# A start-up, a scan entry and a last output reordered in a four-layer convolution and attention kernel

## The chip, the cores and the metric

The kernel runs on one core of a Trainium2 chip, as one program. The metric is device time in microseconds of that core. The kernel before took 3007.63 us, the median of three runs (3004.27 to 3009.06). The engines are named as in the profile: PE (TensorE: matmul), PEld (its weight load), DVE (VectorE), ACT (ScalarE), POOL (GpSimd) and SP (SyncE, which here only issues DMAs). ACT issues DMAs too; an issue takes its place in ACT's own order of instructions.

## The reference

The input x is 8 images of 128 channels and 16 x 16 pixels (256 positions). Four layers follow each other:

- Layer 0: `x = x + adder2d(gn(x), W)`. gn normalises groups of 4 channels (32 groups) over the positions of an image. The adder is a 3 x 3 convolution with a distance in place of the product: `out[f] = -sum |W[f] - patch|` over 128 channels and 9 taps.
- Layer 1: a layer norm over channels, a projection to 2 x 256 channels, and three Mamba branches (forward, backward, in slices). Each takes a causal convolution of 4 taps, SiLU, a projection to a step width (delta, through softplus) and to B and C, and a selective scan of 16 states: `h = exp(delta*A)*h + delta*u*B; y = sum(h*C) + u*D`. Attention between the branches and two 3 x 3 convolutions close it.
- Layer 2: attention within an image and a mixture of 8 experts, two of them chosen.
- Layer 3: a performer of 8 layers, and a spectral layer (convolutions with 16 filters, and a sum over 3 taps) whose result is added to the state and is the output.

## The kernel before

All is fp32. Channels lie on the 128 partitions; the 8 images of 256 positions are 2048 columns, in 4 blocks (pairs of images) of 512. An fp32 matmul shows as two passes in the profile, so that one call of `E.mm` is two PE instructions.

**Layer 0** (`adder_layer`, to about 950 us). It uses |a - b| = 2 max(a, b) - a - b for some taps and |a - b| on ACT for the others. For each of the 128 filters, DVE (L450, L446) and ACT (L452) write a tile d of 128 x 2048 for each tap, from four buffers each, and PE sums d over the channels into a row of `o` (L454 to L458): `add` issues four matmuls of 32 columns, one for each block, into four groups of 32 output partitions. Two sums that depend on no filter pair are left: `px`, the sum over channels of the shifted inputs of six taps (L423 to L425), and `wsum`, the weights' sums (twelve passes: six taps with one output column each, L427). Both are read at L461 to L466, after two filters. `px` and `wsum` come ahead of the first `o` product on PE.

Ahead of these stands `start` (L315): for each pair of images DVE sums x (L333), PE averages over the group (mu), ACT writes the negative mean and the squares (L337, L339), DVE sums the squares (L341), PE averages (var), ACT takes the root (L345), DVE the reciprocal and two scalings into `shifted[1]` (L347 to L350), and copies of it give `shifted[0]` and `shifted[2]` (L351, L354). Between these PE does products that nobody reads, `meanwhile(n)`, one call being two passes.

The loads are issued at the head of `adder_layer` (L375 to L383): on ACT the first 128 columns of the constants, x's pairs 1 and 3, then, in `load_shared`, the other constants, the vectors and the rows; on SP x's pairs 0 and 2, the adder's weights w, and the weights of layer 1 (`load_weights`).

**Layer 1** begins with `first_unit` (L701) on the first pair and branch. Its order is written by hand: norm, projection, convolution, `pp` into `proj` (L759 to L763), the store of `proj`'s rows and their way back as broadcast B and C (`chunk`), then `pd` (L770), which gives delta over ACT and DVE (L774 to L786), the first decays on ACT (L827) and the first scans on DVE (L909). `spare` (L705) lies in the PSUM bank "acc", of which there is one; the scan's accumulator `acc` (L914) takes the same bank, and starts with the products of L916. The copy of `u` (L788) is the last step; the next unit's convolution (`pconv`) needs it.

The order of PE, DVE, ACT and POOL within each `manual_schedule` block is that of the program. Between the blocks the compiler's scheduler orders: of two instructions of one engine in different blocks, the one that can go first may.

**The end** (`spectral_layer`). The outputs lie in five groups of columns: group 0 (positions 0 to 31 of all images), group 1 (32 to 63), group 2 (64 to 127), and groups 3 and 4 (128 to 255, four images each), with 256, 256, 512, 512 and 512 columns. For each, PE adds three taps (L1874), DVE adds the state X (L1876) into `fin`, which has two buffers, and SP stores it (L1882).

Of the kernel before, what the change touches and what calls it, by code (L numbers as in the profile page):

```python
# [16 lines left out]
P = 128  # L17
B = 8
# [3 lines left out]
NBLK = NT // BLK  # L22
# [201 lines left out]
class Env:  # L224
# [31 lines left out]

    def load_shared(self):
        nc = self.nc
        nc.scalar.dma_start(self.cst[:, P:], self.dram["cst"][:, P:])
        nc.scalar.dma_start(self.vecs, self.dram["vecs"])  # L260
        nc.scalar.dma_start(self.rows, self.dram["rows"].partition_broadcast(P))

    def load_weights(self):
        for k, t in self.w.items():
# [42 lines left out]
MAX_TAPS = (0, 2, 4, 6, 8)  # L307
MORE_TAPS = (7,)
MORE = tuple(r for r in range(FG) if r % 10 in (0, 3, 6))
JOINED = (0, 2)  # L310
PX_TAPS = (4, 7, 0, 6, 2, 8)
# [3 lines left out]
def start(E, pool, psum, x, shifted):  # L315

    nc = E.nc
    spare = psum.tile([P, P], F32, tag="px", name="spare")

    def meanwhile(n):  # L320

        for _ in range(n):
            E.mm(spare, E.ones, E.ones)

    def small(name):
        return pool.tile([P, B], F32, tag=name, name=name)

    s1, neg_mu, s2, rs = (small(n) for n in ("s1", "neg_mu", "s2", "rs"))
    sq = pool.tile([P, B, L], F32, tag="sq", name="sq0")
    pairs = [slice(2 * i, 2 * i + 2) for i in range(NBLK)]  # L330
    meanwhile(6)
    for b in pairs:
        nc.vector.tensor_reduce(s1[:, b], x[:, b, :], AX.X, ALU.add)  # L333
        mu = psum.tile([P, 2], F32, tag="st", name="mu0")
        E.mm(mu, E.c("group"), s1[:, b])
        meanwhile(2 if b is not pairs[-1] else 1)
        nc.scalar.copy(neg_mu[:, b], mu)  # L337
        for i in range(b.start, b.stop):
            nc.scalar.activation(sq[:, i, :], x[:, i, :], AF.Square, bias=neg_mu[:, i : i + 1])  # L339
    for b in pairs:  # L340
        nc.vector.tensor_reduce(s2[:, b], sq[:, b, :], AX.X, ALU.add)  # L341
        var = psum.tile([P, 2], F32, tag="st", name="var0")
        E.mm(var, E.c("group"), s2[:, b])
        meanwhile(1 if b is not pairs[-1] else 2)
        nc.scalar.activation(rs[:, b], var, AF.Sqrt, bias=E.eps, scale=-1.0)  # L345
    for b in pairs:
        nc.vector.reciprocal(rs[:, b], rs[:, b])  # L347
        for i in range(b.start, b.stop):
            dst = shifted[1][:, i, 1:17, :].rearrange("p h w -> p (h w)")
            nc.vector.tensor_scalar(dst, x[:, i, :], neg_mu[:, i : i + 1], rs[:, i : i + 1], ALU.add, ALU.mult)  # L350
        nc.scalar.copy(shifted[0][:, b, 1:17, 1:16], shifted[1][:, b, 1:17, 0:15])  # L351
    for i, b in enumerate(pairs):
        op = nc.vector.tensor_copy if i < 2 else nc.scalar.copy
        op(shifted[2][:, b, 1:17, 0:15], shifted[1][:, b, 1:17, 1:16])  # L354


def adder_layer(E):
# [7 lines left out]
    nc, tc = E.nc, E.tc  # L365
    with ExitStack() as ctx:
# [7 lines left out]

        x = last.tile([P, B, L], F32, tag="x", name="x0")  # L375
        nc.scalar.dma_start(E.cst[:, :P], E.dram["cst"][:, :P])
        for i in range(NBLK):
            two = slice(2 * i, 2 * i + 2)
            (nc.scalar if i % 2 else nc.sync).dma_start(x[:, two, :], E.dram["x"][two].rearrange("b c s -> c b s"))
        w = p.tile([P, 9, P], F32, tag="w", name="w0")  # L380
        nc.sync.dma_start(w, E.dram["adder"])
        E.load_shared()
# [9 lines left out]
        neg = p.tile([P, 2, FG], F32, tag="neg", name="neg")  # L392
# [13 lines left out]
        def tap(k):  # L406
            kh, kw = divmod(k, 3)
            return shifted[kw].rearrange("p b h w -> p b (h w)")[:, :, kh * 16 : kh * 16 + L]

        def add(out, lhsT, src, start, stop, blocks=range(NBLK)):  # L410

            for i in blocks:
                E.mm(out[i * FG : (i + 1) * FG, :], lhsT, src[:, 2 * i : 2 * i + 2, :], start, stop)

        px = ps.tile([P, BLK], F32, tag="px", name="px0")
        xsum = p.tile([P, BLK], F32, tag="xsum", name="xsum")
        with tc.manual_schedule(engines={nc.tensor.engine, nc.vector.engine, nc.scalar.engine}):
            nc.scalar.preload_act_table_set(SQRT)
            start(E, p, ps, x, shifted)

            wsum = [ps.tile([P, 1], F32, tag="st", name="wsum") for _ in range(2)]
            weights = [(pw, taps, k) for pw, taps in zip(wsum, (MAX_TAPS, MORE_TAPS)) for k in taps]
            for n, k in enumerate(PX_TAPS):  # L423
                for i in range(NBLK):
                    add(px, neg[:, int(k in MORE_TAPS), :], tap(k), n == 0, n == len(PX_TAPS) - 1, (i,))  # L425
                    for pw, taps, t in weights[2 * i : 2 * i + 2] if n == 0 else ():
                        E.mm(pw, w[:, t, :], E.ones[:, 0:1], start=t == taps[0], stop=t == taps[-1])  # L427

# [2 lines left out]
        for g in range(NG):  # L433
            out = po.tile([P, BLK], F32, tag="o", name="o")
# [100 lines left out]
def _scans(E, ctx, F):  # L535
# [7 lines left out]
    nc, tc = E.nc, E.tc  # L543
    w_x, w_dt = E.w["xproj"], E.w["dtproj"]
    one = ctx.enter_context(tc.tile_pool(name="l1one", bufs=1, reuse_waits="tile"))
    two = ctx.enter_context(tc.tile_pool(name="l1two", bufs=2, reuse_waits="tile"))
# [154 lines left out]
    def first_unit(k, s, p, new, pre, sig, proj):  # L701
# [29 lines left out]
        t = xn[p] = two.tile([P, UT], F32, tag="xn", name="xn1")  # L731
# [20 lines left out]
        t, pc = sig[:, 0, :], pc.rearrange("p b l -> p (b l)")  # L752
# [15 lines left out]
        for h, (tag, scratch) in enumerate((("f", "ln_xc"), ("cs", "ln_rstd"))):  # L768
            pd = ps.tile([P, UT], F32, tag=tag, name="pd")
            E.mm(pd, w_dt[:, k, h * P : (h + 1) * P], proj[0:DTR, :])  # L770
            one_e = one.tile([P, UT], F32, tag=scratch, name="one_e")
            halves.append((pd, delta[:, h, :], pre[:, h, :], sig[:, h, :], one_e))

        for h, (pd, d, e, r, one_e) in enumerate(halves):  # L774
            db = E.v("db" + s, h)
# [91 lines left out]
    with tc.manual_schedule(engines={nc.tensor.engine, nc.vector.engine, nc.scalar.engine, nc.gpsimd.engine}):  # L867
        new, *rest = tiles()
        got[0].update(new)
        first = first_unit(*units[0], new, *rest)  # L870
        next(first)
        for c in range(2):
            chunk("bs", 0, c)
            chunk("cs", NST, c)
        dbs[0] = three.tile([P, 2, UT], F32, tag="db", name="dbu")
        for h in range(2):
            next(first)
            nc.vector.tensor_mul(dbs[0][:, h, :], new["du"][:, h, :], row("bs", 0))
            decays(h)
            if h == 0:  # L880
                rows_of_c(0)
        inputs(1)
        next(first)
        decays(2)
# [7 lines left out]
    with tc.manual_schedule(engines={nc.tensor.engine, nc.vector.engine, nc.scalar.engine, nc.gpsimd.engine}):  # L892
        for r in range(states):
            i, n = divmod(r, NST)
            k, s, p = units[i]
# [905 lines left out]
def spectral_layer(E, W, out):  # L1801
# [7 lines left out]
    nc, tc = E.nc, E.tc  # L1809
    with ExitStack() as ctx:  # L1810

        def enter(name, bufs, **kw):
            return ctx.enter_context(tc.tile_pool(name=name, bufs=bufs, reuse_waits="tile", **kw))

        ugp = enter("sug", 2)
        two = enter("stwo", 2)
# [7 lines left out]
        groups = []  # L1824
        for i in reversed(range(4)):
            lo, hi = ends[i + 1], ends[i]
            n = min(B, BLK // (hi - lo))
# [6 lines left out]
        def at(tile, offset, *dims):  # L1834
            a = tile[:]
            return bass.AP(a.tensor, a.offset + offset, [list(a.ap[0]), *([s, n] for s, n in dims)])

        for step in range(NK // KG):
# [8 lines left out]
            for b in range(B):  # L1847
                for q in range(2):
                    p4 = pu.tile([P, KG, 2, HL], F32, tag="u", name="p4")

                    taps = at(W.T, step * KG * TW + 1, (TW, KG), (HL + 1 - q, 2), (1, HL))
# [4 lines left out]
            for k in range(KG):  # L1856
                for s in range(2):
                    for j, (i, lo, hi, b0, b1) in enumerate(groups):
# [4 lines left out]
                            start=step == 0 and k == 0 and s == 0,  # L1863
                            stop=False,
# [3 lines left out]
        nc.sync.dma_start(mu, E.dram["Mu"].rearrange("i d t e -> d i t e"))  # L1868
        W.running(E, [mu[:, i].rearrange("p t e -> p (t e)") for i in range(4)])
        X = E.X.rearrange("p (b l) -> p b l", l=L)  # L1870
        for j, (i, lo, hi, b0, b1) in enumerate(groups):
            for k in range(TAPS):
                tap = u[:, b0:b1, TAPS - 1 - k + lo : TAPS - 1 - k + hi]
                E.mm(acc[j], mu[:, i, k, :], tap.rearrange("p b (i q) -> p b q i", q=2), start=False, stop=k == TAPS - 1)  # L1874
            fin = two.tile([P, b1 - b0, hi - lo], F32, tag="fin", name="fin")
            nc.vector.tensor_tensor(  # L1876
                fin.rearrange("p b (i q) -> p b q i", q=2),
                X[:, b0:b1, lo:hi].rearrange("p b (i q) -> p b q i", q=2),
                acc[j],
                ALU.add,  # L1880
            )
            nc.sync.dma_start(out[b0:b1, :, lo:hi].rearrange("b c s -> c b s"), fin)  # L1882


def program(tc, dram, out, cols):
    with ExitStack() as ctx:
        E = Env(ctx, tc, dram, cols)
        adder_layer(E)
        mamba_layer(E)
        E.early.close()  # L1890
        with ExitStack() as tail:
            W = Spectral(E, tail)
            performer_layer(E, W)
            spectral_layer(E, W, out)
# [25 lines left out]
```

## Time and profile before

| | |
|---|---|
| median of three runs | 3007.63 us (3004.27 to 3009.06) |
| profiled execution, its own time | 3000.94 us |
| its span, first to last instruction | 2999.2 us |
| PE busy | 2854.1 us (95%), 16404 instructions |
| DVE busy | 2419.8 us (81%) |
| ACT busy | 2273.2 us (76%) |
| POOL busy | 699.6 us (23%) |
| o products of the adder (L289) | 921.5 us, 8512 passes |
| first s1 sum (L333) starts | 4.02 us |
| first o product starts | 24.83 us |
| first scan (L909) starts | 978.91 us |
| last fin (L1876) starts | 2995.26 us |

Lines of the page give an engine, a line, what is written and read, a count, busy time and the mean of one. "Idle" is what the engine waited just before, with what ended it. L289 is the helper `E.mm`, so matmuls are told apart by their tiles. The chain of work that ended last is followed back from the last instruction. All sums below are made on the profiled execution.

### The profile page before, as it was taken

The page shows a single profiled execution, that of the slowest core. Times are in us where ns is not written, and L with a number is a line of the kernel's source. Part 1 is how long each engine was busy: PE and PEld are TensorE (multiplying, and loading weights), DVE is VectorE, ACT ScalarE, POOL GpSimd, SP SyncE. Part 2 cuts the span into 40 slices and gives each one's busy share as a digit, 9 for nine tenths or more (in the row PEclk, how much of TensorE's full clock was granted, in tenths as well). Part 3 has the DMA queues.
Part 4 walks back from the last instruction along what each step waited for, and adds up shares of the span by engine and source line. Part 5 has one row for each costly group of instructions (what it writes and reads, how often), then busy time and mean ns, then how long its engine had stood idle before and what let it go on. Part 6 is the DMA issues. An engine that isn't in the chain of part 4 may idle for free.

```text
span 2999.2 us, 41845 instructions
## 1 busy us (share of the span) xinstructions
PE 2854.1 (95%) x16404; PEld 1275.4 (43%) x16404; DVE 2419.8 (81%) x3398; ACT 2273.2 (76%) x2744; POOL 699.6 (23%) x415
## 2 busy tenths in 40 slices
PE   9999999999999788998898998999999999999999
PEld 4222222222223333443343454455655555654444
DVE  8999999999997999999899658887777787784110
ACT  8999999999997777778777435578778778777332
POOL 0000000000000889998999400000000000000100
PEclk9999999999999999999999999999999999999999
DMA  2000000000000444344344200000000000001100
GB/s 68 1 1 5 1 1 5 1 2 5 1 1 16 169 149 148 135 149 141 133 157 137 84 29 1 14 1 14 14 14 1 14 14 1 14 1 53 43 29 14
DMA packets 39482, 133.46 MB, mean 44 GB/s; under 512 B 7522, under 2 KB 10732, under 8 KB 37748
## 3 DMA queue, kind: packets, MB, share of 16 engines
q1 hardware_dynamic: 38164, 129.46, 12.5%
q8 instruction: 129, 2.11, 0.3%
q10 hardware_dynamic: 1120, 1.32, 0.1%
q14 instruction: 69, 0.57, 0.1%
HBM read 127.88 MB, written 1.84 MB: 43 GB/s over the span
## 4 chain that ended last, share of the span: by engine, by line
PE 70%; DVE 16%; ACT 7%; POOL 3%; issue 3%; DMA 1%; DVEq 0%; ACTq 0%; POOLq 0%
PE o L289 30%; PE p L289 10%; DVE st L909 5%; PE acc L289 5%; PE g L289 4%; PE conv L289 3%; PE pc L289 2%; PE var L289 2%; PE pf L289 2%; POOL dbu L814 2%; PE pq L289 2%; PE pconv L289 1%; PE pn L289 1%; PE pa L289 1%; ACT da L827 1%
## 5 line engine op out<-in xcount | busy, mean ns | idle before, releaser
L289 PE MATMUL o<-d,sel 128*32 128x512 f32 x8512 | 921.5, 593 | 2.1 <-DVE d L446 1.2
L452 ACT ACTIVATE d<-sh,w 128x2048 f32<-128x2048 f32 x472 | 899.3, 1993 | 25.4 <-PE o L289 25.1
L450 DVE TENSOR_SCALAR d<-sh,w 128x2048 f32<-128x2048 f32 x592 | 718.4, 1281 | 11.0 <-PE o L289 10.9
L814 POOL TENSOR_TENSOR dbu<-du,bs 128x1024 f32<-128x1024 f32 x191 | 446.4, 2363 | 975.6 <-DVE du L786 970.1
L289 PEld LDWEIGHTS o<-d,sel 128*32 128x32 f32 x8512 | 278.6, 110 | 644.2 <-issue 523.0
L909 DVE TENSOR_TENSOR_SCAN st<-da,dbu 128x512 f32<-128x512 f32 x384 | 446.2, 1206 | 17.9 <-POOL dbu L814 13.8
L289 PE MATMUL acc<-st,cst 128*128 128x512 f32 x768 | 375.4, 621 | 52.8 <-DVE st L920 52.6
L827 ACT ACTIVATE da<-delta,neg_a 128x510 f32<-128x510 f32 x384 | 256.8, 684 | 79.1 <-DVE st L909 73.8
L289 PEld LDWEIGHTS acc<-st,cst 128*128 128x128 f32 x768 | 144.6, 196 | 252.7 <-issue 144.0
L920 DVE TENSOR_TENSOR st<-st,pcs 128x1024 f32<-128x1024 f32 x168 | 205.2, 1221 | 18.9 <-ACT pcs L819 1.6
L446 DVE SCALAR_TENSOR_TENSOR d<-sh,w,d 128x2048 f32<-128x2048 f32 x88 | 206.8, 2350 | 1.9
L1855 ACT COPY ug<-p 128x512 f32<-128x512 f32 x128 | 74.9, 585 | 136.7 <-PE p L289 136.7
L1173 ACT ACT_TABLE_LOAD x134 | 171.9, 1283 | 2.4
L1396 POOL TENSOR_TENSOR lw<-lw,turn 128x640 f32<-128x640 f32 x8 | 10.0, 1255 | 685.6 <-DVE turn L1395 592.6
L819 ACT COPY pcs<-cs 128x512 f32<-128x512 f32 x168 | 97.7, 582 | 54.2 <-DVE st L920 48.4
L289 PE MATMUL conv<-pad,f 128*128 128x512 f32 x288 | 135.0, 596 | 0.9 <-ACT pad L1071 0.5
L289 PE MATMUL p<-un,lw 128*128 128x512 f32 x256 | 123.7, 605 | 3.8 <-DVE un L1467 2.1
L289 PE MATMUL p<-g,lw 128*128 128x512 f32 x256 | 116.4, 597 | 3.9 <-ACT g L1181 3.9
L289 PE MATMUL p<-T,H 128*128 128x512 f32 x256 | 113.0, 600 | 0.8 <-DVE H L1784 0.8
L289 PE MATMUL g<-ug,me 128*128 128x512 f32 (+1 forms) x320 | 112.0, 509 | 0.0
L1181 ACT ACTIVATE ex<-ex 128x352 f32<-128x352 f32 x128 | 62.4, 494 | 51.6 <-DVE ex L1664 50.4
L289 PE MATMUL pf<-lw,rk 128*128 128x352 f32 x256 | 97.2, 476 | 0.5 <-DVE ek L1614 0.3
(366 smaller groups left out, 3898.6 us busy)
## 6 DMA issues: line engine op xcount, KB each, us to landing
bs<-rows SPq DMA_DIRECT2D x96, 512.0 KB, 3.8
cs<-rows SPq DMA_DIRECT2D x96, 512.0 KB, 4.6
m<-in_Mphi SPq DMA_DIRECT2D x8, 1024.0 KB, 4.9
lw<-in_layers SPq DMA_DIRECT2D x8, 948.0 KB, 4.7
f<-in_fuse SPq DMA_DIRECT2D x2, 1152.0 KB, 9.9
T<-in_T SPq DMA_DIRECT2D x1, 2064.0 KB, 7.4
diag<-in_diag SPq DMA_DIRECT2D x1, 1920.0 KB, 7.5
total<-sums SPq DMA_DIRECT2D x16, 64.0 KB, 2.0
```

The costliest lines, as they stand in the source:

```text
L289: self.nc.tensor.matmul(out, lhsT=lhsT, rhs=rhs, start=start, stop=stop)
L446: nc.vector.scalar_tensor_tensor(d, tap(k), wk, d, ALU.max, ALU.add)
L450: nc.vector.tensor_scalar(d, tap(k), wk, None, ALU.max)
L452: nc.scalar.activation(d, tap(k), AF.Abs, scale=-1.0, bias=wk)
L814: nc.gpsimd.tensor_tensor(dbs[r], got[r // NST]["du"], bc(row("bs", r), 1, 2), ALU.mult)
L819: nc.scalar.copy(pcs[r], row("cs", r))
L827: nc.scalar.activation(das[g % 3][:, :, 1:], d[:, :, 1:], AF.Exp, scale=a)
L909: nc.vector.tensor_tensor_scan(st[:, h, :], da, dbs[r][:, h, :], 0.0, ALU.mult, ALU.add)
L920: nc.vector.tensor_tensor(st, st, bc(pcs[r][:, :], 1, 2), ALU.mult)
L1173: S.tc.keep_in_program_order(S.nc.scalar.preload_act_table_set(name))
L1181: S.nc.scalar.activation(out, src, func, **kw)
L1855: nc.scalar.copy(dst, p4)
```

## The change

Six edits:

1. x is loaded in eight pieces of one image each, the even ones from SP and the odd ones from ACT, in place of four pairs.
2. The other constants, the vectors and the rows are issued from SP, behind x and w.
3. The last two unread products of `start` (after the fourth var) are left out.
4. The weights' sums are all issued ahead of px; px no longer takes the blocks one by one in its first tap.
5. `first_unit` issues 13 unread products (26 passes) behind the two `pd`.
6. The output groups are finished in the opposite order: 4, 3, 2, 1, 0.

```diff
     def load_shared(self):
         nc = self.nc
-        nc.scalar.dma_start(self.cst[:, P:], self.dram["cst"][:, P:])
-        nc.scalar.dma_start(self.vecs, self.dram["vecs"])
-        nc.scalar.dma_start(self.rows, self.dram["rows"].partition_broadcast(P))
+        nc.sync.dma_start(self.cst[:, P:], self.dram["cst"][:, P:])
+        nc.sync.dma_start(self.vecs, self.dram["vecs"])
+        nc.sync.dma_start(self.rows, self.dram["rows"].partition_broadcast(P))
...
         E.mm(var, E.c("group"), s2[:, b])
-        meanwhile(1 if b is not pairs[-1] else 2)
+        meanwhile(1 if b is not pairs[-1] else 0)
...
-        for i in range(NBLK):
-            two = slice(2 * i, 2 * i + 2)
-            (nc.scalar if i % 2 else nc.sync).dma_start(x[:, two, :], E.dram["x"][two].rearrange("b c s -> c b s"))
+        for b in range(B):
+            (nc.scalar if b % 2 else nc.sync).dma_start(x[:, b, :], E.dram["x"][b])
...
-        def add(out, lhsT, src, start, stop, blocks=range(NBLK)):
+        def add(out, lhsT, src, start, stop):
 
-            for i in blocks:
+            for i in range(NBLK):
                 E.mm(out[i * FG : (i + 1) * FG, :], lhsT, src[:, 2 * i : 2 * i + 2, :], start, stop)
...
-            weights = [(pw, taps, k) for pw, taps in zip(wsum, (MAX_TAPS, MORE_TAPS)) for k in taps]
+            for pw, taps in zip(wsum, (MAX_TAPS, MORE_TAPS)):
+                for k in taps:
+                    E.mm(pw, w[:, k, :], E.ones[:, 0:1], start=k == taps[0], stop=k == taps[-1])
             for n, k in enumerate(PX_TAPS):
-                for i in range(NBLK):
-                    add(px, neg[:, int(k in MORE_TAPS), :], tap(k), n == 0, n == len(PX_TAPS) - 1, (i,))
-                    for pw, taps, t in weights[2 * i : 2 * i + 2] if n == 0 else ():
-                        E.mm(pw, w[:, t, :], E.ones[:, 0:1], start=t == taps[0], stop=t == taps[-1])
+                add(px, neg[:, int(k in MORE_TAPS), :], tap(k), n == 0, n == len(PX_TAPS) - 1)
...
             halves.append((pd, delta[:, h, :], pre[:, h, :], sig[:, h, :], one_e))
+        meanwhile(13)
...
-        for j, (i, lo, hi, b0, b1) in enumerate(groups):
+        for j, (i, lo, hi, b0, b1) in reversed(list(enumerate(groups))):
             for k in range(TAPS):
```

## The prediction

> **What bounds the kernel now.** I read the chain of work that ended last first, by stages, because the edits touch four short stretches: 0 to 26 us, 968 to 983 us, and the last 15 us.
>
> The start, in that chain (start us, length us, what):
>
> ```profile
> 13.83 1.06 PE spare L289 x4
> 14.89 1.85 PE px L289 x2
> 16.74 0.82 PE wsum L289 x4
> 17.56 0.98 PE px L289 x2
> 18.53 0.54 PE wsum L289 x4
> 19.07 0.97 PE px L289 x2
> 20.04 0.54 PE wsum L289 x4
> 20.58 4.84 PE px L289 x41
> ```
>
> TensorE carries the chain from 9.9 us on, and after px come the o products back to back: over the whole adder stage o sat idle 2.1 us (the page's first group). DVE had its four d tiles ready at 21.1 and then waited 5.84 us for o; ACT waited 3.67. So every us by which px ends earlier is a us of the kernel, until px ends before about 19 us, where DVE's tiles are no longer there.
>
> Why the norm ahead of it is late, from the timeline:
>
> ```profile
> 5.14 0.33 ACTq L261 DMA_DIRECT2D rows<-in_rows  x1
> 5.51 1.28 ACT L418 ACT_TABLE_LOAD   x1 [5.51 <-DMA x<-in_x]
> 9.03 0.69 DVE L333 TENSOR_REDUCE s<-x 128x2 f32<-128x512 f32 x1 [2.60 <-DMA x<-in_x]
> ```
>
> Two delays: ACT's table load stands behind six DMA issues (rows goes out at 5.14, with the landing of the second x piece at 5.12; vecs at 3.42, with the landing of cst at 3.41; SP's fifth issue at 4.01, its first landing at 4.02: a queue seems to have four loads under way), and the fourth x pair lands only at 9.0, 7.3 us after its issue, where the others took 3.3 to 3.9.
>
> The Mamba entry, again in the chain:
>
> ```profile
> 968.09 0.43 PE spare L289 x2
> 968.52 0.04 issue
> 968.57 1.12 PE acc L289 x2
> 969.69 1.07 PE pd L289 x2
> ...
> 981.44 0.52 ACT u L788
> 981.96 0.04 issue
> 982.00 5.98 PE pconv L289 x8
> ```
>
> proj is ready at 968.71 (copy at 968.13, 0.58), yet pd starts at 969.62 by the timeline: the two acc products of L916, emitted later in the program, have slipped in ahead of it.
>
> The clock there, by stages (the last three columns are granted clock, DMA share, GB/s):
>
> ```profile
> 972.00:974.00 2.00, 0.66 (x2) 0.00 (x0) 1.48 (x4) 1.48 (x4) 0.00 (x0) 0.75 1.06 260
> 974.00:982.00 8.00, 0.00 (x0) 0.00 (x0) 7.79 (x12) 3.57 (x7) 0.42 (x1) 0.50 0.54 181
> 982.00:986.00 4.00, 4.00 (x5) 1.85 (x6) 3.86 (x5) 1.83 (x3) 4.00 (x2) 0.50 0.13 49
> ```
>
> The clock halves at 973.0 and comes back at 986.7; pconv runs at half speed.
>
> **What the skill says.** "TensorE: Matmul & The Clock Gate", Part 1: the array is at half clock by default or after an idle window of about 3.4 us, and at full clock after a busy one; the windows run free. The trace agrees: 128x512 passes start 0.85 us apart at 982 and 0.43 later, and the changes at 973.0, 986.7, 1075.4, 1078.8 lie multiples of 3.41 us apart. Carried back, that grid gives 17.3 us, where px changes from 1.92 to 1.05 us a pair. "DMA: Bandwidth & Descriptors", queues, rings and completion order: each DMA engine takes turns between queues, packet by packet. This fits the late x pair: w's rows of 4.6 KB on SP's queue against x's of 1 KB; from 5 to 7 us SP's queue moved 0.55 MB and ACT's 0.19. "TensorEngine Tiling (Array Packing)", key properties: a change of tiling mode drains the array; px is 128x32 and wsum 128x128, and each wsum's weight load after a px sat idle 0.84 us.
>
> **The change, part by part.**
>
> *Loads.* Eight pieces of 128 KB replace four of 256. DMA moved 0.38 MB/us from 3 us on, 0.2 MB before. With equal packets on both queues (cst's 128 are 0.5 KB), pair 0 needs 0.46 MB: 3.9 us; pairs 1 and 2: 4.6 and 5.3. The last piece is ACT's fifth load, issued at 3.42 when cst has landed; w waits on SP for x's first landing (3.9), so it reaches the engines about when x is done; behind it on SP stand only loads of the next sentences. I take 6.5 us (5.8 to 8) for pair 3, against 9.0. w (0.59 MB, behind it) lands at about 7.3, needed at 10.9. cst, vecs and rows go behind it on SP; first needed at 36 us (L466, L469), in POOL's center (nothing waits until 952) and at 946 us. Cost nothing; weights for 952 us and later have 900 us.
>
> *ACT.* One issue after 3.42 instead of two: table load 3.8 to 5.1, neg_mu at 5.1 instead of 6.80. ACT takes 0.985 us a pair: pairs end at 6.2, 7.2, 8.2, 9.15; before, 11.56. DVE's last s2 ends at 9.9, not 12.28 (-2.4), then its own order (four times reciprocal and two scalings, 0.85) gives sh1 complete at 13.3 and the first d at 13.9 against 16.21. ACT's copies of sh0 end at 13.9.
>
> *TensorE.* var3 ends at 10.9 (before 13.84). Removed: two spare products, 0.86 us, hidden since. Moved: 12 wsum passes at about 0.2 us (cold, 0.82 for four) = 2.5 us: 10.9 to 13.4, in the time in which DVE and ACT scale; their cover is sh1 at 13.3. px then starts at 13.4 with all four blocks: in four column groups, 48 passes at 0.1075 (0.43 us for four) = 5.16 us at full clock. Tap 4, before, took 5.7 us from 14.89 to 20.58 in single groups between the sums; now 0.86. But the clock: wsum has one column and counts for little, as var and spares between 10.4 and 13.8 left it cold. From 13.4 dense, a window must fall in: 2.6 to 6.1 us at half speed, a loss of 1.3 to 3.0; I take 2.1. px ends at 13.4 + 5.16 + 2.1 = 20.7, against 25.3 (the last px starts at 25.26). **-4.6 us** (-3.8 to -5.4 by the clock; a pair 3 at 8.0 costs 1.3 of it). DVE has four tiles by 18.8, so it is not the bound.
>
> *Spares ahead of the scan.* 13 products are 26 passes at 0.11 (16 took 1.95) = 2.8 us on TensorE, where it idles 9.35 us before pconv; cover 9.35, nothing waits for them. They hold the bank "acc" of spare longer, so L916's acc can't go ahead of pd: it goes behind the spares, where only the state sums of 987.8 need it. pd starts at 968.76, not 969.62: **-0.86** (bounds 0 and -0.9), and ACT's Abs, DVE's chain and the first scan (978.91) with it; bs's landing (970.49 + 3.8) is early enough. The clock: spares and acc end at about 975.2, u is copied at 981.1, 5.9 us idle. Windows with 25 to 30% activity took the clock down (973.0, 1147.1); some window in such a gap is emptier, so pconv stays cold: 0. Were it warm, 2.4 us less (8 passes, six of them 0.43 shorter).
>
> *Last outputs.* Products keep their sum. Order is now 512, 512, 512, 256, 256 columns; the last addition takes 0.42 instead of 0.69: -0.27. But fin has two buffers, and the last (columns 0 to 31) takes that of group 2, whose output has 256 B rows and landed 2.6 us after issue: issue at 2993.04, landing 2995.64; TensorE is ready at 2995.26. Nothing is queued behind it on DVE but its own store waits. So +0.40, together **+0.13** (-0.27 to +0.4). Its own landing: 2.3 us, as the last one now.
>
> Sum on the profiled execution: -4.6 - 0.86 + 0.13 = -5.3; span 2999.2 to 2993.9. Its own time was 3000.94, 6.7 under the median shown. In other runs the windows fall elsewhere: before, the dense stretch 13.7 to 16.6 is only 2.9 us long, so a window that misses it leaves px of blocks 1 and 2 cold too, and px ends up to 5 us later (a gain that the new order would not lose). I add 0.2 for that: 3007.6 - 5.5 = **3002.1 us**. 0.2% (6.0 us) is about what a measurement can tell from no change.
>
> **Rivals.**
>
> 1. *More (3000 to 2997):* the median run is one with the late clock before (3 to 5 us more gain), or pconv is warm (2.4). For: all three runs shown lie 3.3 us or more above the profiled one. Against: one trace gives the threshold only narrowly.
>
> 2. *Nearly nothing (3004 to 3007.6):* the clock's loss is at its 3.0, pair 3 lands at 8, and acc still slips ahead of pd: -4.6 + 0.9 + 1.3 = -2.4, and less if wsum waits for w. This is also the case that the change doesn't do what it says.
>
> 3. *Slower (3008 to 3014):* the last image on ACT's queue is starved by w as the fourth pair is now. If it again needs 7.3 us it lands at 10.7 and px ends at 24.7, still 0.6 early. It decides from 11.3 us for this stretch, 12.0 with the Mamba part; at 16 us the kernel is 4 us slower. Against: it is half the bytes, and w itself is issued 2.2 us later than now.
>
> **How the numbers follow.** Forecast 0.58 (3.5 to 7.5 us saved: 3000.1 to 3004.1), rival 1 0.17, rival 2 0.17, rival 3 0.08. The range 2998.9 to 3006.9 leaves out rival 3, and the ends of 1 and 2. Over 6.0 us faster: 0.4 of the forecast and most of rival 1, with the spread of the runs 0.42; slower by over 6: 0.05; between: 0.53.
>
> **What would show it.** Right: table load at 3.8, fourth s1 at 6 to 8, twelve wsum passes in one row ending near 13.4, px in rows of four, first o product at 20 to 21.5; pd straight after the proj copy, with acc behind 26 spare passes; pconv's first passes 0.85 apart; the last fin idle on a DMA for about 0.4 us. Wrong: s1 idle beyond 9 us, wsum waiting on w, px cold past 19.5, or o waiting for DVE's d after px.

## The result, and the profile after

| | before | changed |
|---|---|---|
| median (range), beside each other on one chip | 3006.16 us (2999.53 to 3009.37) | 2999.18 us (2994.85 to 3004.92) |
| ratio | | 0.9978, 95% interval 0.9971 to 0.9985 |
| profiled execution, own time / span | 3000.94 / 2999.2 us | 3004.53 / 3002.7 us |
| first d of DVE starts | 16.21 us | 16.10 us |
| first o product starts | 24.83 us | 23.07 us |
| proj copy to first scan | 10.78 us | 9.91 us |
| first product of the last sums to the end of the span | 15.35 us | 15.74 us |

The change saves 7.0 us (0.23%; by the interval 4.5 to 8.7), where 5.5 were forecast. The profiled execution of the kernel before was among its shortest and that of the changed kernel among its longest, so the two spans are not compared; the stretches around the edits are.

The start, in the chain of work that ended last of the changed kernel (start us, length us, what):

```profile
13.51 0.22 PE var L289 x2
13.72 2.56 PE wsum L289 x12
16.28 6.96 PE px L289 x48
23.24 5.14 PE o L289 x45
```

The twelve sums stand in one row and px in another, as written. In this chain TensorE now needs 9.5 us from the end of var to the end of px; before, 12.0 (13.83 to 25.85). But the var that begins it still ends at 13.7. The reason is in the timeline of DVE and ACT:

```profile
3.54 1.28 ACT L417 ACT_TABLE_LOAD   x1 [3.54 <-DMA cst<-in_cst]
3.93 0.69 DVE L333 TENSOR_REDUCE s<-x 128x2 f32<-128x512 f32 x1 [3.93 <-DMA x<-in_x]
6.36 1.41 DVE L333 TENSOR_REDUCE s<-x 128x2 f32<-128x512 f32 x2 [1.74 <-DMA x<-in_x]
8.92 0.69 DVE L333 TENSOR_REDUCE s<-x 128x2 f32<-128x512 f32 x1 [1.15 <-DMA x<-in_x]
```

The table load came forward from 5.51 to 3.54 us. The x did not: the second pair is later than before (5.14), and the last begins at 8.92, not 9.03.

The Mamba entry, in TensorE's timeline of the changed kernel:

```profile
966.83 2.12 PE L289 MATMUL pd<-proj,w_dtproj 8*128 8x512 f32 x4 [0.25 <-ACT proj L761]
968.88 4.62 PE L289 MATMUL spare<-cst 128*128 128x128 f32 x26
973.55 1.98 PE L289 MATMUL acc<-uc,diag 128*128 128x512 f32 x4
979.20 5.15 PE L289 MATMUL pconv<-u,diag 128*128 128x512 f32 x8 [3.67 <-ACT u L787]
```

pd now waits for ACT's copy of proj alone, and all four acc passes stand behind the 26 unread ones. These took 4.62 us, not the 2.8 forecast, but nothing waits for them. The clock there, by stages (granted clock, DMA share and GB/s last):

```profile
974.00:976.00 2.00, 1.54 (x4) 0.38 (x2) 1.93 (x4) 1.28 (x2) 0.00 (x0) 1.00 1.00 401
976.00:978.00 2.00, 0.00 (x0) 0.00 (x0) 1.97 (x4) 0.05 (x1) 0.00 (x0) 1.00 0.17 68
978.00:980.00 2.00, 0.80 (x1) 0.50 (x2) 1.86 (x3) 2.00 (x4) 1.22 (x1) 0.69 0.00 0
980.00:982.00 2.00, 2.00 (x4) 0.75 (x3) 1.97 (x3) 1.03 (x2) 2.00 (x2) 0.50 0.00 0
```

It halves at about 978.8, before pconv. The tail, in DVE's timeline:

```profile
2996.89 0.42 DVE L1876 TENSOR_TENSOR fin<-X,g 128x256 f32<-128x256 f32 x1 [0.77 <-PE g L289]
2998.94 0.42 DVE L1876 TENSOR_TENSOR fin<-X,g 128x256 f32<-128x256 f32 x1 [1.62 <-DMA out_y<-fin]
```

The last addition waits 1.62 us for an output's landing, where all five waited for TensorE before.

### The profile page after: what moved, and what is told of

The parts are those of the page before. It is cut to its first block, busy times and chain, and to the rows that moved or that the text cites. A ratio compares the mean times of both kernels' runs of the same rounds, so it can differ in the third digit from the quotient of the medians.

```text
span 3002.7 us, 41899 instructions
## 1 busy us (share of the span) xinstructions
PE 2863.5 (95%) x16426; PEld 1278.1 (43%) x16426; DVE 2422.0 (81%) x3398; ACT 2274.2 (76%) x2744; POOL 699.6 (23%) x415
## 3 DMA queue, kind: packets, MB, share of 16 engines
HBM read 127.88 MB, written 1.84 MB: 43 GB/s over the span
## 4 chain that ended last, share of the span: by engine, by line
PE 71%; DVE 14%; ACT 7%; POOL 4%; issue 3%; DMA 1%; ACTq 0%; DVEq 0%; POOLq 0%
PE o L289 30%; PE p L289 10%; PE acc L289 5%; DVE st L908 4%; PE g L289 4%; PE conv L289 4%; POOL dbu L813 2%; PE pc L289 2%; PE var L289 2%; PE pf L289 2%; PE pq L289 2%; PE pconv L289 1%; PE pn L289 1%; PE pa L289 1%; PE px L1670 1%
```

## The experiments

The theory was the prediction's: the start gives nearly all, by x's earlier arrival and by px's order. After the traces it was in doubt, since x had not come earlier. The expectations call it A. Three rivals stood: it is px's order alone, at the size that the two traces show, about 2.5 us (B); it is px's order, whose larger worth is in executions where the clock of the kernel before comes late (C); or the gain is luck of the clock in the later stages (D).

The first seven kernels are cut, so that a few us can be seen: they have the loads, the norm, px, the sums and the first 6 of 128 filters of layer 0, and store the state then; layers 1 to 3 are left out. The four that follow are whole, and so is the second look at the kernel before. The first four cut kernels ran together on one chip, six executions each (four with the loads of before); the other three ran together on another chip, so a difference between the two sets is less certain than one within a set.

### The whole start, in the cut kernel

The cut of the kernel before, and the cut of the changed kernel:

> Cut short: only the loads, the start, px, the weights' sums and the first 6 of 128 filters of layer 0 are computed, then X from them is stored; layers 1 to 3 are left out. Start in the form of the kernel before. It is the yardstick of the next three: about 65 to 80 us, and a spread of 1 to 5 us between its own runs if the place of the clock's free-running window matters.

> The same cut, start in the form of the changed kernel. Theory A (the prediction's size: loads and sums together): 4.6 us shorter than the cut kernel before, and the fourth s1 sum starts at 6 to 8 us in its trace. Theory B (what the one trace of the changed kernel shows: pairs landed at 6.3 and 8.9 us, so that only the moved sums count): 2.6 us shorter. Theory C (the clock: the order before often misses the window that brings full clock): 5 us or more, with a narrower spread than the cut kernel before.

Before: 81.76 us median, in two groups (76.56, 76.77; 81.33, 82.19, 82.41, 82.64). Changed: 76.57 (75.66 to 77.23), in one. So the start is worth 5.2 us in the medians, and the gain is there with all later stages left out (against D as the only cause). It is a little over A's 4.6, but the fourth sum of x, which A wanted at 6 to 8 us, starts at 9.61. The kernel before has executions 5 us longer than others, which the changed one has not: this is C's sign.

### Each half of it undone

The changed cut with the loads of before:

```diff
-        for b in range(B):
-            (nc.scalar if b % 2 else nc.sync).dma_start(x[:, b, :], E.dram["x"][b])
+        for i in range(NBLK):
+            two = slice(2 * i, 2 * i + 2)
+            (nc.scalar if i % 2 else nc.sync).dma_start(x[:, two, :], E.dram["x"][two].rearrange("b c s -> c b s"))
```

(and the three constants on ACT again)

> The same cut, changed kernel with the loads of before (pairs, other constants from ACT). A: 2.3 us longer than the cut changed kernel. B: within 0.4 us of it. C: within 0.4 us of it.

The changed cut with px and the sums in the order of before:

```diff
-            for n, k in enumerate(PX_TAPS):
-                add(px, neg[:, int(k in MORE_TAPS), :], tap(k), n == 0, n == len(PX_TAPS) - 1)
+            for n, k in enumerate(PX_TAPS):
+                for i in range(NBLK):
+                    add(px, neg[:, int(k in MORE_TAPS), :], tap(k), n == 0, n == len(PX_TAPS) - 1, (i,))
+                    for pw, taps, t in weights[2 * i : 2 * i + 2] if n == 0 else ():
+                        E.mm(pw, w[:, t, :], E.ones[:, 0:1], start=t == taps[0], stop=t == taps[-1])
```

(and the blocks in `add`, the list `weights` and the two last unread products of the norm again)

> The same cut, changed kernel with px by blocks between the weights' sums and the two unread products ahead, as before. A: 2.3 us shorter than the cut kernel before. B: 0.1 us shorter. C: no shorter, and as widely spread as the cut kernel before.

With the old loads 75.18 us (74.7 to 75.6): the new loads cost 1.4 us, which none of the three theories had expected. With the old order 83.32, again in two groups (76.84, 78.05; 82.94 to 84.16): the new order saves 6.7, and with the old loads 6.6 (81.76 to 75.18). The groups go with px's order, whatever the loads. Within the short group the order is worth only some 1.5 us (76.7 to 75.2), less than B's 2.6. The other 5 us are in the longer group. "The order" here takes in the two unread products left out ahead of px, which stood for 1.06 us in the chain of the kernel before; no run takes them out alone.

### Is the longer group the clock?

The cut of the kernel before with 14 unread products more ahead of px:

```diff
-        meanwhile(1 if b is not pairs[-1] else 2)
+        meanwhile(1 if b is not pairs[-1] else 16)
```

> The cut kernel before with 16 unread products (32 passes) instead of 2 behind the fourth var, just ahead of px: 14 products more on TensorE's path. If the clock is what spreads and lengthens the order before: the products open a window of full clock themselves in 2.6 to 6.1 us, so px and the sums run at full clock in every run: 80.2 us (79.3 to 81.2), in one group, below the 81.8 of the cut kernel before although it does more. If it isn't the clock: 14 products at 0.21 to 0.43 us more than the cut kernel before, 84 to 88 us, and still in two groups.

81.09 us (80.83 to 81.55, four executions), in one group, and 0.7 under the median without the 14 products on the other chip. TensorE's timeline of this kernel (start, busy):

```profile
13.97 5.08 PE L289 MATMUL spare<-ones 128*128 128x128 f32 x32
18.98 1.04 PE L289 MATMUL px<-sh,neg 128*32 128x512 f32 x2
19.95 0.61 PE L289 MATMUL wsum<-ones,w 128*128 128x1 f32 x4
```

5.1 us of dense products, of which 4 are added work, and px is at full clock from its first pair (1.04 us; at half clock 1.9). Adding work that nobody reads removed the longer group, as a cause in the clock would have it; a cause in the loads or in the order of the work would have left it, and added the 4 us. The profiled executions of the two cut kernels that fall in two groups are both of the short group, so the longer one needs a trace of the whole kernel.

### The late clock in the whole kernel

The kernel before once more, for another trace:

> The kernel before once more, for a second trace of it. Theory (the clock comes late in most executions of the order before): if its own time is at 3004 us or more, px and wsum, which ended at about 25.4 us in the first trace, end at 27 to 31 us in this one, with the passes of the first blocks 0.85 us apart, and the rest of the kernel shows no loss of that size. Rival (the executions differ by the clock's halvings in the later stages): px ends at 25 to 26 us whatever the time, and the difference stands after 100 us. At an own time under 3002 us the trace tells nothing between the two.

Its own time was 3005.20 us, and this trace has the late clock. The chain of work that ended last:

```profile
15.06 1.85 PE px L289 x2
16.91 0.94 PE wsum L289 x4
17.85 1.84 PE px L289 x2
19.70 0.94 PE wsum L289 x4
20.64 1.84 PE px L289 x2
22.48 0.94 PE wsum L289 x4
23.43 7.35 PE px L289 x41
30.78 0.01 PE o L289 x3
```

Beside the lines shown of the first trace: every pair of px takes 1.84 us and every four sums 0.94, where these were 0.97 and 0.54 from 17.6 us on, and 41 passes take 7.35, not 4.84. The first o product starts at 30.19 us, 5.36 later. Nothing takes that back in the adder: the first unread product behind it starts at 953.64, 5.28 after the 948.36 of the first trace. So C is shown, with its size, in one trace against another. In the changed kernel's trace the same product starts at 945.77, 2.6 us ahead of one trace of the kernel before and 7.9 ahead of the other.

The changed start has a spread of its own. The changed kernel without the 13 products (told of below) has the same start, and its trace shows (TensorE):

```profile
15.00 0.43 PE L289 MATMUL var<-s,cst 128*128 128x2 f32 x2
15.29 2.70 PE L289 MATMUL wsum<-ones,w 128*128 128x1 f32 x12
17.92 8.00 PE L289 MATMUL px<-sh,neg 128*32 128x512 f32 x48
...
948.36 2.27 PE L289 MATMUL spare<-cst 128*128 128x128 f32 x18
```

Here the last sum of x starts only at 10.62 us, px takes 8.00, and the adder ends level with the first trace of the kernel before, 5.3 us ahead of the second.

Nor is D nothing. From this product to the end of the span it is 2050.8 and 2049.8 us in the two traces of the kernel before, 2050.4 in the one just shown, but 2056.9 in the changed kernel's: that execution won 2.6 to 7.9 us at its start and lost 6 to 7 behind the adder. A part of it is at 2678.6, where this trace has 6.8 us at half clock that neither trace of the kernel before has, and loses 2.8 us. How such losses fall in the medians is not shown.

### Why x came no earlier

Three arrangements of the loads, on the changed cut. x by pairs, on two queues, with the constants still on SP (the edit of the loads above, without the constants):

> The cut changed kernel with x by pairs on two queues, the other constants on SP as changed. If w's long rows on SP starve the images on ACT: within 0.7 us of the cut changed kernel (76.6). If the single images are what slows the loads: near the cut kernel with the loads of before, 75.2 or below.

76.86 us (73.53 to 77.53), as the changed cut. The four sums of x start at 3.97, 5.40 (two) and 10.23. This kernel and the one with the loads of before (75.18; last sum at 8.31) differ in the place of the constants alone. And all pairs on SP, ahead of w, with only the first constants on ACT:

```diff
-        for b in range(B):
-            (nc.scalar if b % 2 else nc.sync).dma_start(x[:, b, :], E.dram["x"][b])
+        for i in range(NBLK):
+            two = slice(2 * i, 2 * i + 2)
+            nc.sync.dma_start(x[:, two, :], E.dram["x"][two].rearrange("b c s -> c b s"))
```

> The cut changed kernel with x by pairs, all four on SP ahead of w; ACT loads only the first constants. If two queues sharing the engines are what delays the later pairs: pairs land at 3.5, 4.2, 5.0 and 5.8 us, the fourth var comes 2 us earlier than with the loads of before, 73 to 73.8 us. If not: 75 us or above.

74.58 us (71.56 to 75.3): 2.0 under the changed cut, a little less than expected. All four sums now run without a pause:

```profile
4.10 2.91 DVE L333 TENSOR_REDUCE s<-x 128x2 f32<-128x512 f32 x4 [4.10 <-DMA x<-in_x]
```

The queues (q1 is SP's, q10 ACT's) show two separate losses. From 4 to 5 us, first the kernel before, then the changed one:

```profile
DMA packets 384, 0.38 MB, mean 376 GB/s; under 512 B 31, under 2 KB 380, under 8 KB 384
q1 hardware_dynamic: 222, 0.23, 63.9%
q10 hardware_dynamic: 162, 0.15, 45.1%
```

```profile
DMA packets 177, 0.17 MB, mean 169 GB/s; under 512 B 12, under 2 KB 177, under 8 KB 177
q10 hardware_dynamic: 92, 0.09, 32.5%
q1 hardware_dynamic: 85, 0.08, 23.1%
```

With single images the queues ran part empty between 3 and 5 us: 0.21 and 0.17 MB a us here and 0.20 to 0.30 in three other traces, against 0.34 to 0.42 in ten traces with pairs. The prediction's "four loads under way" on a queue does not hold: with all pairs on SP, that queue issued seven loads by 3.81 us, ahead of its first landing (4.1). What the issues of the traces fit is eight loads under way on both queues together: in the changed kernel the ninth (ACT's fourth image, 3.17) waited for the first load to land and the tenth (w, 3.36) for the second. With single images these eight are half as large. That this is the cause of the gap is argued from the issue times, not tried by itself; and what the gap costs no run shows, since pairs on two queues, which have no gap, were no faster. The second loss is the long rows on SP, of w and of the constants behind it: from 7 to 8 us, SP's queue moved 0.39 MB in the changed kernel and ACT's 0.01; with x by pairs and the constants on SP the last x pair, on ACT, got 0.05, 0.13 and 0.06 MB in the three us from 5 on, and its sum started only at 10.23. Put on one queue ahead of w, x is summed by 7.0.

### The spare products ahead of the scan, and the best loads in the whole kernel

The changed kernel without `meanwhile(13)`:

> The changed kernel without the 13 spare products behind pd. Theory (they keep acc behind pd): acc stands ahead of pd again, pd starts about 1.5 us after the copy of proj starts, not 0.63, and the first scan comes 0.9 us later against that copy; the whole kernel 0.9 us slower than the changed one if nothing else follows (about 3000), more if the halved clock meets pconv. Rival (the products' worth is the clock): the clock halves earlier in the gap and pconv takes 6 us and more, where the changed kernel showed 5.15; then 1.5 to 2 us slower. A difference under 2 us is not seen in the medians, only in the trace.

2998.28 us (2994.19 to 3005.32; ratio 0.9985, 0.9975 to 0.9995, to the kernel before beside it), not to be told from the changed kernel. TensorE's timeline:

```profile
968.50 1.12 PE L289 MATMUL acc<-uc,diag 128*128 128x512 f32 x2
969.56 1.98 PE L289 MATMUL pd<-proj,w_dtproj 8*128 8x512 f32 x4
971.47 1.12 PE L289 MATMUL acc<-uc,diag 128*128 128x512 f32 x2
981.94 5.61 PE L289 MATMUL pconv<-u,diag 128*128 128x512 f32 x8 [9.35 <-ACT u L786]
```

acc is ahead of pd again, and from the copy of proj to the first scan it is 10.78 us, as in both traces of the kernel before; with the products 9.91. pconv took 5.61 us here, 5.98 and 5.15 in the traces before and after: half clock at its start in all of them.

The changed kernel with x by pairs on SP (the edit of the cut kernel above):

> The changed kernel with x as four pairs, all on SP ahead of w, the constants still on SP behind it, ACT with only its first load. By the cut kernels: 2.0 us faster than the changed kernel, about 2997 (2994 to 3000), with the four sums of x at 4.1 to 7.0 us without a pause and the last var at about 12.3, px ending at about 22.5. If the start's gain is lost on the way (the adder stage bound elsewhere), it stands at the changed kernel's 2999.

2993.78 us (2987.39 to 2997.64), against 3004.59 of the kernel before beside it: ratio 0.9968 (0.9960 to 0.9976), 9.6 us by the ratio. This is faster than the kernel before, and by the medians than the changed kernel too, though the intervals of the two ratios touch and the two did not run side by side. Its shortest executions, 2987.4 and 2987.5, are of a kind not met before; the first was profiled. TensorE's timeline:

```profile
4.67 0.38 PE L289 MATMUL mu<-s,cst 128*128 128x2 f32 x2 [0.63 <-DVE s L333]
10.01 0.35 PE L289 MATMUL var<-s,cst 128*128 128x2 f32 x2
10.23 1.63 PE L289 MATMUL wsum<-ones,w 128*128 128x1 f32 x12
11.79 7.16 PE L289 MATMUL px<-sh,neg 128*32 128x512 f32 x47
```

The clock was full from the first mean to the sums (a mean shows 0.38 us, at half clock 0.59; wsum took 1.63, not 2.70): the last var comes at 10.01, the first d at 13.80, the first o product at 18.45. In px it was lost for a while: the granted clock is 0.50 from 12 to 14 us, and px took 7.16. The start is half of this execution's gain. Its span is 13.6 us shorter than that of the first trace of the kernel before; 6.6 of them stand at the end of the adder (941.77), the other 7.0 come behind it (2043.8 us, where five of the six others have 2049.7 to 2050.8).

With the last output tile in memory of its own besides:

```diff
-            fin = two.tile([P, b1 - b0, hi - lo], F32, tag="fin", name="fin")
+            fin = (two if j else one).tile([P, b1 - b0, hi - lo], F32, tag="fin" if j else "fin_last", name="fin")
```

> As the kernel with all x pairs on SP, and the last output tile in memory of its own, so that its addition waits for no output's landing. Theory: the idle time of the last addition on an output (1.62 us in the changed kernel, of which TensorE's products would have left about 1.2) goes; from the first of the last products to the end 15.35 us or a little less, against 15.74; the whole 0.4 us under the kernel without it, not to be seen in the medians. If the last addition then waits for TensorE all the same, the tail stays at 15.7.

2994.51 us (2989.73 to 3001.0; ratio 0.9970, 0.9958 to 0.9983), not told from the last. The last addition, in DVE's timeline:

```profile
2992.17 0.42 DVE L1877 TENSOR_TENSOR fin<-X,g 128x256 f32<-128x256 f32 x1 [1.04 <-PE g L289]
```

It waits for TensorE again, 0.58 us less. From the first product of the last sums to the end it is 15.03 us; 15.61 with the wait, 15.35 in the kernel before. This execution began at half clock (all sums of x by 7.0 us, yet the first d only at 15.01), and px took 8.16 us, so that its adder ends at 945.72, no earlier than the changed kernel's (945.77): the earlier x was lost in px.

Last, twelve unread products in place of six ahead of the norm:

```diff
-    meanwhile(6)
+    meanwhile(12)
```

> The kernel with all x pairs on SP, and twelve in place of six unread products ahead of the first group mean (12 more passes). Theory (a start at half clock is what px and the norm pay for, and a dense stretch of over 5 us ahead of them brings the full clock): the first mean of x starts at 5.5 to 6.5 us, not 4.7, but the clock is 1.0 by then or soon after; first d at about 15.0 as before, px in rows of 0.43 us for the most part, first o at 19.5 to 22 us, not 23.1; the whole kernel about 2.5 us faster than the kernel with six, about 2991.3 (2990 to 2994), its fastest runs no faster than that kernel's 2987.4. Rival (the clock is lost again among the small products of the norm, and the longer start only delays): px cold as before, first o at 23 to 24 us, the kernel 0.5 to 1.5 us slower than the one with six, 2994.5 to 2995.5.

2995.78 us (2990.37 to 2997.05; ratio 0.9965, 0.9952 to 0.9979), not told from the kernel with six, so the 2.5 us are not shown and the medians lean to the rival. Its trace has half of each. TensorE's timeline:

```profile
5.35 0.28 PE L289 MATMUL mu<-s,cst 128*128 128x2 f32 x2
10.59 0.35 PE L289 MATMUL var<-s,cst 128*128 128x2 f32 x2
10.80 2.51 PE L289 MATMUL wsum<-ones,w 128*128 128x1 f32 x12
13.24 8.00 PE L289 MATMUL px<-sh,neg 128*32 128x512 f32 x48
```

The norm ran at full clock and its last var came at 10.59, but the clock was lost again among the small products: wsum took 2.51 us and px 8.00.

## Why the prediction was right in the total, and where not

**Loads (-2.4): wrong.** The failing step is "I take 6.5 us (5.8 to 8) for pair 3": its sum starts at 8.92 us, and the loads alone cost 1.4 us in the cut kernel instead of saving. In the traces the cost is less sure: the last sum of x starts at 8.92, 9.50, 9.61 and 10.62 with single images, at 8.31, 8.35, 9.03, 9.20 and 9.31 with the loads of before, 0.8 us later in the mean. Three assumptions failed. "DMA moved 0.38 MB/us from 3 us on" was taken over to loads of half the size, where it was 0.17 to 0.30. w was taken to reach the engines when x is done, but it was issued at 3.36, not 3.9, and its rows took the engines while ACT's images were still open. And the constants on SP were to "cost nothing", but put long rows behind w's. This is rival 3's mechanism. Its 10.7 us for the last image were met in one trace (10.62), though not the 11.3 from which it decides.

A second thing was left out of that step. Even with x in by 7.0 us, the first d came at 15.0, not 13.9, when the clock was half; at full clock, 13.80. ACT's squares wait for the means, and TensorE, with two unread products between any two means at half clock, gives one only every 1.28 us. The prediction set ACT's pace at 0.985 us a pair and looked for no wait between.

**wsum hidden in the scaling: not quite.** Its 2.5 us measured 2.6 to 2.7. It ends at 16.28, while DVE has scaled the last pair at 15.5, 1.8 us after the last var and not the 2.4 forecast: some 0.7 us of it stands on the chain. The two unread products left out, priced at nothing ("hidden since"), were in that chain before, for 1.06 us.

**px in four groups with a clock loss of 2.1: right.** From the end of var to the first o product 9.8 us were forecast (10.9 to 20.7), and 9.5 measured; 48 passes took 6.96, a loss of 1.8 on 5.16. In the other traces with this order at half clock px took 7.5 to 8.2, a loss of up to 3.0, which was the forecast's own bound.

**The late clock of the kernel before (+0.2): right in mechanism, undersized.** "px ends up to 5 us later" measured 5.36. But the prediction weighted it as an exception, though the median shown lay 6.7 us over the profiled execution. In the cut kernels it was 4 of 6 executions, in both kernels with the old order. The sentence in rival 1 that spoke for it was the one to follow.

**Mamba entry (-0.86): right.** -0.87, by the displaced acc, shown by taking the 13 products away. pconv stayed cold at its start, as forecast, but the reason given, "windows with 25 to 30% activity took the clock down", is not read from the trace for 973.0: in the 3.4 us ahead of it TensorE shows as busy for 90% (31% ahead of 1147.1). The figure needs pd's products of 8 rows not to count; no run tries that.

**Tail (+0.13):** +0.39 in the two traces. The shorter last addition gave -0.32 (15.35 to 15.03; forecast -0.27), and the wait for group 2's output cost 0.58, not 0.40: its landing took 2.7 us. The 0.13 that are missing lie between one trace with this order and another (15.74 and 15.61).

The sum from the runs: px's order -6.6 and loads +1.4 (medians of the cut kernels), entry -0.87 and tail +0.39 (traces) make -5.7, inside the interval of -8.7 to -4.5. The forecast of -5.5 had -4.6 for the start, with the wrong halves: a load gain of 2.4 that was a loss of about 1, and a clock gain of some 5 us, in four executions of six, counted as 0.2. That the total was met is luck: these two errors nearly cancel. The saving of 7.0 us lies at the far end of the forecast's own 3.5 to 7.5 and beyond the 6.0 us taken as the bound of no change, so that the smaller of the two main chances (faster, 0.42) came true; with the late clock sized as it is, it would have been the larger. How often the whole kernel before has the late clock is known only from its spread and two traces, so the share of each part in 7.0 us stays a share of medians.

## What to carry to other kernels

A trace is one draw: where its time lies several us under the median, look for the stretch that the clock's timing could lengthen (sparse products ahead of a dense row that sets the end) and size it as part of the median, not as an exception. In this kernel the loads that the first work waits for came soonest on one queue, ahead of anything with longer rows; moving the other loads behind them on one queue was not enough while the other queue still had some of them to bring. When an engine is to start earlier, check each handover of the chain at the pace that the chain really has, unread products at half clock included.

## What was not expected of the hardware

- 14 products that nobody reads, 4 us of added work, made the median of the cut kernel 0.7 us shorter (81.09 against 81.76, on two chips) and its spread 0.7 us instead of 6.
- In the first 20 us the granted clock by stages does not show the half clock reliably: for the changed kernel it gave 1.00 from 14 to 20 us, where px's passes of a block started 0.85 us apart until 19.6. Where an earlier change is on record it does show: 0.50 from 8 us on in the second trace of the kernel before. The spacing of equal passes is the safer reading.
- With loads of half the size, the same bytes of x and the same queues, the rate between 4 and 5 us fell from 0.38 to 0.17 MB a us, and in three other traces to 0.20 to 0.30.
- An earlier x need not bring an earlier end: with all of x summed by 7.4 us the adder ended at 941.77, 943.73 and 945.72 in three traces, by the clock that px met.
